# A two-layer decoder on one core: which VectorE instruction the sums of the experts are queued behind in linear attention

## The chip, the cores and the metric

The kernel runs on one core of one Trainium2 chip. The metric is the device time of one execution in microseconds; the time before is the median of three runs. Engines are named as the profile names them: PE is TensorE (PEld its weight loads), DVE is VectorE, ACT is ScalarE, POOL is GpSimd, SP is SyncE, which here only issues DMAs.

## The reference

A decoder of two layers works on x of 16 batch items, 256 positions and 256 features, in float32. Each of its six sublayers adds to x a function of the layer-normalised x:

```python
x = x + _L0_attn_ref(_layernorm(x, axis=-1), ...)    # causal softmax attention
x = x + _L0_xattn_ref(_layernorm(x, axis=-1), ctx_1024, ctx_1024, ...)
x = x + _L0_ffn_ref(_layernorm(x, axis=-1), ...)     # 8 experts, the best 2 of each token
x = x + _L1_attn_ref(_layernorm(x, axis=-1), ...)    # linear attention
x = x + _L1_xattn_ref(_layernorm(x, axis=-1), ctx_1024, ctx_1024, ...)
x = x + _L1_ffn_ref(_layernorm(x, axis=-1), ...)     # gated experts in the values and the output
```

The change lies where the third meets the fourth. The third ends with a sum: each token adds the outputs of its two experts, weighted. The fourth is linear attention with 16 heads of 16 features and the feature map phi(x) = elu(x) + 1:

```python
q, k, v = (_phi(qkv[0]), _phi(qkv[1]), qkv[2])
# for each position t:
S = S + k_t[..., :, None] * v_t[..., None, :]
z = z + k_t
out_t = einsum('bhde,bhd->bhe', S, q_t) / maximum(sum(z * q_t), 1e-6)
```

The kernel computes the same as a causal product: scores q k over all earlier positions, without a softmax, times v, divided by the row's sum.

## The kernel before

The program is one long unrolled sequence. x stays in SBUF as sixteen tiles `xs[b]` of 128 partitions by 2 by 256. Stages follow one another: attention and cross attention (layer 0), the experts (72 tiles of 128 gathered tokens, each result written to the DRAM tensor `yd`), then linear attention, cross attention and gated experts (layer 1). TensorE's instructions stand in the order in which the program writes them (`tc.manual_schedule`); those of the other engines are put in order by a scheduler when the program is built, by their dependences and its own estimate of when each is ready. Every engine's queue is then fixed, and each instruction waits there for its inputs. `tc.issue_after(i)` adds, to each instruction written in its block on the engine of `i`, the demand that it stands behind `i` in that queue. It adds no other dependence; instructions of the block on other engines are free.

Linear attention runs in steps s. A batch item b has four, one for each `(m, o)`: m is a half of the heads, o every second head of it, so step s works on item s // 4. `step3` writes, in this order: the scores of step s (`scores3`, L1014); the product with the values of step s - 2 (`weighted3`, L1030 and L1035); the transposition and division of step s - 3 (`finish3`, L1046 and L922 to L924); in even steps `project3` for step s + 2 (L197), which makes queries and keys for two steps; in steps 4b + 1 the transposition of the scaled rows of item b + 1 (`rows3`, L972) and the output projection of item b - 2 (`output3`); in steps 4b + 2 `combine(b + 2)`; in steps 4b + 3 the transposition of the result of item b - 1 (`out_T`) and the values of item b + 1 (`values3`). Into this the program fills the keys and values that cross attention needs later, made from the context (`context4`, the tile `c` loaded at L79 by SP, results stored by SP at L296 and L303): eight pieces ahead of the first step, three in each step before 0, and one in each later step.

Three pieces touch the change.

- `combine(b)` gathers, for each half t of item b and each of its two experts r, the rows of `yd` into a tile `y` (an indirect DMA issued by POOL, L949, four buffers), adds them weighted to `xs[b]` on DVE (L953, four sums), takes the statistics (L142, L143), the reciprocal standard deviation in twelve small instructions (L171 and L152 to L160), and scales the rows into `h` (L962, two instructions). `rows3(b)` reads `h`.
- `project3(b, m)` multiplies into PSUM, ACT takes exponential and relu of it (L998, L999), DVE forms `qk = min(ex, 1) + relu` (L1000), which is phi, and ACT makes the masked keys `ks` from it (L1003).
- `scores3` writes two PSUM tiles `sc`, of which there are two in all, so the next step's scores need both emptied: ACT copies one whole (L1023) and the middle of the other (L1022), DVE masks the rest of the other (L1021), and POOL later masks the first in SBUF (L1024).

A fourth piece is moved by it. `load_ffn` is written after step 10: two POOL copies (L895) that read a few elements of `xs[2]`, and behind them twelve SP loads of the last stage's weights (L899, L902).

Before, the block of `combine` is put behind the last instruction of the previous `combine`:

```python
with ExitStack() as order:
    if last:
        order.enter_context(tc.issue_after(last[-1]))
    ...
last.append(done.ins)
```

Of the kernel before, what the change touches and what calls it, by code (L numbers as in the profile page):

```python
# [13 lines left out]
ALU = mybir.AluOpType  # L14
# [11 lines left out]
def decoder(ctx: ExitStack, tc: tile.TileContext, a: dict, out: bass.AP):  # L26
# [3 lines left out]
    nc = tc.nc  # L30
# [108 lines left out]
    def stats(layer, b, pool):  # L139
        st = pool.tile([P, 2, 6], F32, tag="bnst", name="bnst", bufs=2)  # L140
        for t in range(2):
            nc.vector.bn_stats(st[:, t, :], xs[b][:, t, :])  # L142
            nc.vector.bn_aggr(mvs[layer][:, 2 * b + t, :], st[:, t, :])  # L143
# [22 lines left out]
    def rstd_one(layer, b, pool, eng=nc.vector):  # L166

        if layer not in rstds:
            rstds[layer] = const.tile([P, NT], F32, tag=f"rstd{layer % 2}", name=f"rstd{layer}")
        v = pool.tile([P, 2], F32, tag=f"rs_v{layer % 2}", name="rs_v", bufs=2)  # L170
        nc.vector.tensor_scalar(v, mvs[layer][:, 2 * b : 2 * b + 2, 1], 1e-5, None, ALU.add)  # L171
        rsqrt(rstds[layer][:, 2 * b : 2 * b + 2], v, pool, eng)
# [21 lines left out]
    def two_k(ps, lhsT, rhs):  # L194

        for c in range(2):
            nc.tensor.matmul(ps, lhsT=lhsT(c), rhs=rhs(c), start=(c == 0), stop=(c == 1))  # L197
# [731 lines left out]
    with ExitStack() as st:  # L929
# [2 lines left out]
        stats_tile(3)  # L932
        stats_tile(4)
        hs3, hTs, ons, qks, ats, oss = {}, {}, {}, {}, {}, {}
        last = []

        def mm3(shape, name):
            return psum.tile(shape, F32, tag="mm", name=name, bufs=4)

        def combine(b):  # L940

            with ExitStack() as order:
                if last:
                    order.enter_context(tc.issue_after(last[-1]))
                for t in range(2):
                    i = 2 * b + t
                    for r in range(2):
                        y = pool.tile([P, D], F32, tag="y", name="y", bufs=4)
                        nc.gpsimd.indirect_dma_start(  # L949
                            out=y, out_offset=None, in_=yd,  # L950
                            in_offset=bass.IndirectOffsetOnAxis(ap=rows[:, i, r : r + 1], axis=0),
                        )
                        nc.vector.scalar_tensor_tensor(  # L953
                            xs[b][:, t, :], y, gates[:, i, r : r + 1], xs[b][:, t, :],
                            ALU.mult, ALU.add,
                        )
                stats(3, b, pool)
                rstd_one(3, b, pool)
                h = hs3[b] = hp.tile([P, 2, D], F32, tag="h", name="h")
                for t in range(2):  # L960
                    i = 2 * b + t
                    done = nc.vector.tensor_scalar(  # L962
                        h[:, t, :], xs[b][:, t, :], mvs[3][:, i, 0:1], rstds[3][:, i : i + 1],
                        ALU.subtract, ALU.mult,
                    )
            last.append(done.ins)

        def rows3(b):
            ps = mm3([P, 2, S], "ps_hT")
# [20 lines left out]
        def project3(b, m):  # L990
            ps = mm3([P, 2, S], "ps_qk")
            for i in range(2):
                cols = slice(i * D + m * P, i * D + (m + 1) * P)
                two_k(ps[:, i, :], lambda c: wlqk[:, c, cols], lambda c: hTs[b][:, c, :])

            ex = pool.tile([P, 2, S], F32, tag="ex", name="ex", bufs=1)
            qk = pool.tile([P, 2, S], F32, tag="qk", name="qk", bufs=2)
            nc.scalar.activation(ex, ps, AF.Exp)  # L998
            nc.scalar.activation(qk, ps, AF.Relu)  # L999
            nc.vector.scalar_tensor_tensor(qk, ex, 1.0, qk, ALU.min, ALU.add)  # L1000
            ks = pool.tile([P, 2, S], F32, tag="ks", name="ks", bufs=2)
            for i in range(2):
                nc.scalar.mul(ks[:, i, :], qk[:, 1, :], halves[:, i : i + 1])  # L1003
            qks[b, m] = qk, ks

        def scores3(b, m, o):
            qk, ks = qks[b, m]
            at = ats[b, m, o] = pool.tile([P, 4, 3, P], F32, tag="at", name="at", bufs=3)
            scs = [psum.tile([P, 2, 512], F32, tag="sc", name="sc", bufs=2) for _ in range(2)]
            for cols, out_cols in ((slice(0, S), slice(0, S)), (slice(P, S), slice(S, S + P))):  # L1010
                k0 = cols.start
                for j in range(4):
                    part = slice(32 * j, 32 * j + 32)
                    nc.tensor.matmul(  # L1014
                        scs[j // 2][:, j % 2, out_cols], lhsT=ks[part, o, k0 : k0 + P],
                        rhs=qk[part, 0, cols], start=True, stop=True,
                    )
            sc3 = [x[:, :, 0:384].rearrange("p j (a q) -> p j a q", a=3) for x in scs]
            tri = tri3[:, 0::2, :].unsqueeze(1).to_broadcast([P, 2, 2, P])

            nc.vector.tensor_tensor(at[:, 0:2, 0::2, :], sc3[0][:, :, 0::2, :], tri, ALU.mult)  # L1021
            nc.scalar.copy(at[:, 0:2, 1, :], sc3[0][:, :, 1, :])  # L1022
            nc.scalar.copy(at[:, 2:4], sc3[1])  # L1023
            nc.gpsimd.tensor_tensor(at[:, 2:4, 0::2, :], at[:, 2:4, 0::2, :], tri, ALU.mult)  # L1024
# [55 lines left out]
        def step3(s):  # L1080
            def at_(k):
                return SETS[k] if 0 <= k < len(SETS) else None

            if at_(s):
                scores3(*SETS[s])
            if at_(s - 2):
                weighted3(*SETS[s - 2])
            if at_(s - 3):
                finish3(*SETS[s - 3])
            b = s // 4  # L1090
            if s % 2 == 0 and at_(s + 2):
                project3(*SETS[s + 2][:2])
            if s % 4 == 1:
                if b + 1 < NB:
                    rows3(b + 1)
                if b - 2 >= 0:
                    output3(b - 2)
            if s % 4 == 2 and 0 <= b + 2 < NB:
                combine(b + 2)
            if s % 4 == 3:  # L1100
                if 0 <= b - 1 < NB:
                    out_T(b - 1)
                if b + 1 < NB:
                    values3(b + 1)

        with tc.manual_schedule(engines={mybir.EngineType.PE}):
            next(late[0])
            next(late[1])
            combine(0)
            fill(late, 8)  # L1110
            for s in range(-3, len(SETS) + 6):
                step3(s)
                fill(late, 3 if s < 0 else 1)
                if s == 10:
                    load_ffn(xs[2][0:1, 0, 0:32])
# [391 lines left out]
```

## Time and profile before

| what | value |
|---|---|
| median of three runs | 3912.89 us (3911.7 to 3913.84) |
| profiled execution | 3917.66 us, span 3916.0 us |
| granted TensorE clock, mean | 0.983 |
| DVE busy in the span | 57% |
| last matmul of the experts to first scores of linear attention | 2016.7 to 2064.28 us |
| scores of step 0 to step 12 | 2064.28 to 2127.65 us |
| step 16 to step 56 | 2145.80 to 2341.50 us |
| ACT waiting for L1000, 2100 to 2350 us | 53.3 us in 25 waits |
| L1000 | 32 instructions, median 0.69 us |
| L953 | 64 instructions, median 0.48 us, longest 1.49 us |

Times within the kernel are microseconds from the start of the span. In a line of the timeline the first number is the start, the second the length, then engine, source line, operation, output and inputs; `x8` counts instructions that were merged, and what stands in square brackets is how long the engine had been idle and what ended that. In the chain of waits each piece is what the next one had to wait for. The clock is the share of full speed that TensorE was granted in a stretch.

### The profile page before, as it was taken

What the parts mean: (1) busy time and instruction counts of PE and PEld (TensorE: products, weight loads), DVE (VectorE), ACT (ScalarE), POOL (GpSimd) and SP (SyncE); (2) the same over time, 40 slices, a digit from 0 to 9 for tenths busy, and PEclk for the clock granted to TensorE, in tenths of its full rate; (3) what the DMA queues carried; (4) which work ended last, traced back from release to release, by engine and by line L of the source; (5) the groups of instructions that cost most, each with busy time, mean ns of one, the idle gap of its engine ahead of it and who ended that gap; (6) DMA issues with size and microseconds to landing.
All of it is one profiled execution on the core that took longest, in us unless ns stands there. A gap on an engine that the chain in (4) does not pass through costs nothing.

```text
span 3916.0 us, 63635 instructions
## 1 busy us (share of the span) xinstructions
PE 3759.0 (96%) x23088; PEld 2679.1 (68%) x23088; DVE 2248.7 (57%) x6215; ACT 1616.7 (41%) x4876; POOL 1039.2 (27%) x1472
## 2 busy tenths in 40 slices
PE   8999999999999999979989888998999999999999
PEld 6777776777777776756667665665666666666666
DVE  5666667645556555522234765776655555555554
ACT  4555554555555555423335555665212212212211
POOL 3332332333344334322224653221100000000000
PEclk9999999999999999979999999999999999999999
DMA  5000000010000000032234001001222222222222
GB/s 192 1 1 1 1 1 1 1 57 17 9 17 17 17 9 17 17 89 65 64 122 146 28 17 35 25 26 24 56 64 58 65 64 58 65 64 58 66 63 49
DMA packets 88456, 171.65 MB, mean 44 GB/s; under 512 B 12480, under 2 KB 60744, under 8 KB 79952
## 3 DMA queue, kind: packets, MB, share of 16 engines
q1 hardware_dynamic: 78992, 148.65, 13.9%
q0 software_dynamic: 8576, 17.87, 1.7%
q8 instruction: 186, 3.05, 0.3%
q10 hardware_dynamic: 576, 1.05, 0.1%
q14 instruction: 126, 1.03, 0.1%
HBM read 139.70 MB, written 27.82 MB: 43 GB/s over the span
## 4 chain that ended last, share of the span: by engine, by line
PE 86%; DVE 9%; issue 2%; ACT 1%; DMA 1%; POOL 1%; SPq 0%; another core or an unknown queue 0%; ACTq 0%; DVEq 0%; POOLq 0%
PE ps_qk L197 14%; PE po L1412 11%; PE ps_ve L197 11%; PE ps_v L197 6%; PE tr L266 6%; PE po L503 6%; PE sc L235 4%; PE ps_h L197 3%; PE po L877 3%; PE av L272 3%; PE sc L431 2%; PE av L488 2%; PE sc L1231 2%; PE sc L1205 2%; PE zt L1244 1%
## 5 line engine op out<-in xcount | busy, mean ns | idle before, releaser
L256 POOL TENSOR_TENSOR pr<-pr,sm 128x256 f32<-128x256 f32 (+1 forms) x384 | 309.7, 827 | 1444.2 <-DVE sm L254 1337.5
L250 ACT ACTIVATE pr<-sc,nmx 128x128 f32<-128x128 f32 (+1 forms) x768 | 314.7, 417 | 348.1 <-DVE nmx L248 311.9
L1412 PE MATMUL po<-w_oe,ut 128*128 128x256 f32 x2048 | 452.4, 379 | 0.0
L197 PE MATMUL ps_ve<-w_ve,hT 128*128 128x512 f32 x1024 | 450.8, 593 | 0.0
L1412 PEld LDWEIGHTS po<-w_oe,ut 128*128 128x128 f32 x2048 | 388.8, 190 | 52.8 <-issue 0.2
L267 ACT COPY pT<-tr 128x512 f32<-128x512 f32 (+1 forms) x256 | 135.9, 531 | 650.2 <-PE tr L266 650.2
L266 PEld LDWEIGHTS tr<-ident,pr 128*128 128x128 f32 x2176 | 270.8, 141 | 168.5 <-issue 117.5
L266 PE MATMUL tr<-ident,pr 128*128 128x128 f32 x2176 | 346.8, 275 | 14.1 <-ACT zT L497 11.2
L452 POOL TENSOR_TENSOR pr<-pr,sm 128x512 f32<-128x512 f32 x256 | 264.2, 1053 | 286.8 <-DVE sm L450 176.4
L446 ACT ACTIVATE pr<-sc,nmx 128x256 f32<-128x256 f32 x512 | 236.7, 470 | 250.8 <-DVE nmx L441 172.3
L197 PEld LDWEIGHTS ps_ve<-w_ve,hT 128*128 128x128 f32 x1024 | 191.1, 190 | 215.3 <-issue 207.1
L1384 DVE TENSOR_TENSOR tv<-ps_ve,gm 128x512 f32<-128x512 f32 x256 | 176.4, 689 | 204.7 <-PE ps_ve L197 198.2
L441 DVE CUSTOM_DVE_ANT_0 sc<-sc,mk 128x256 f32<-128x256 f32 x512 | 211.0, 443 | 112.6 <-PE sc L431 59.5
L248 DVE TENSOR_REDUCE nmx<-sc 128x2 f32<-128x256 f32 (+1 forms) x384 | 208.2, 556 | 111.0 <-ACT pr L250 106.2
L197 PE MATMUL ps_qk<-hT,w_a 128*128 128x256 f32 x1024 | 260.0, 387 | 0.0
L267 DVE COPY pT<-tr 128x384 f32<-128x384 f32 (+1 forms) x384 | 223.0, 594 | 19.2 <-PE tr L266 12.9
L197 PEld LDWEIGHTS ps_qk<-hT,w_a 128*128 128x128 f32 x1024 | 180.8, 191 | 29.7 <-issue 11.8
L197 PE MATMUL ps_qk<-hT,w 128*128 128x256 f32 x768 | 194.0, 398 | 0.0
L866 DVE COPY hs<-ps_h 128x512 f32<-128x512 f32 x72 | 49.8, 691 | 223.0 <-PE ps_h L197 223.0
L1211 DVE TENSOR_REDUCE nm<-sc 128x4 f32<-128x1024 f32 x128 | 150.9, 1221 | 43.2 <-PE sc L1205 43.2
L235 PE MATMUL sc<-qk 64*128 64x128 f32 (+1 forms) x1536 | 163.4, 346 | 8.6 <-ACT qk L417 6.2
L197 PEld LDWEIGHTS ps_qk<-hT,w 128*128 128x128 f32 x768 | 147.5, 203 | 19.4 <-issue 1.2
(279 smaller groups left out, 7010.4 us busy)
## 6 DMA issues: line engine op xcount, KB each, us to landing
gr<-gd SPq DMA_DIRECT2D x128, 512.0 KB
yd<-y SPq DMA_DIRECT2D x72, 128.0 KB
c<-in_ctxT SPq DMA_DIRECT2D x32, 256.0 KB
m_w<-in_m_w SPq DMA_DIRECT2D x16, 512.0 KB
x<-in_x SPq DMA_DIRECT2D x16, 256.0 KB
mk<-in_mask SPq DMA_DIRECT2D x16, 256.0 KB
hd<-h SPq DMA_DIRECT2D x16, 256.0 KB
w_ve<-in_f_ve SPq DMA_DIRECT2D x8, 512.0 KB
```

The lines of the kernel that those rows point to most:

```text
L197: nc.tensor.matmul(ps, lhsT=lhsT(c), rhs=rhs(c), start=(c == 0), stop=(c == 1))
L235: nc.tensor.matmul(sc[:, j, at : at + ks], lhsT=qk[rows, 0, qs], rhs=qk[rows, 1, 0:ks], start=True, stop=True,)
L248: nc.vector.tensor_reduce(nmx[:, qt, :], sc[:, :, sl], AX.X, ALU.max, negate=True)
L250: nc.scalar.activation(pr[:, j, sl], sc[:, j, sl], AF.Exp, bias=nmx[:, qt, j : j + 1], accum_out=sm[:, qt, j : j + 1],)
L256: nc.gpsimd.tensor_tensor(pr[:, :, sl], pr[:, :, sl], sm[:, qt, :].unsqueeze(2).to_broadcast([P, 2, n]), ALU.mult,)
L266: nc.tensor.transpose(tr[:, at : at + P], src, ident)
L267: copy(pT, tr[:, 0 : P * len(blocks)])
L441: nc.vector.tensor_tensor_reduce(out=sc[:, j, t, :], in0=sc[:, j, t, :], in1=mk[:, t, :], scale=-1.0, scalar=3.4e38, op0=ALU.add, op1=ALU. ...
L446: nc.scalar.activation(pr[:, j, t, :], sc[:, j, t, :], AF.Exp, bias=nmx[:, j, t : t + 1], scale=-1.0, accum_out=sm[:, j, t : t + 1],)
L452: nc.gpsimd.tensor_tensor(pr[:, j], pr[:, j], sm[:, j, :].unsqueeze(2).to_broadcast([P, 2, S]), ALU.mult)
L503: nc.tensor.matmul(po, lhsT=zTs[l, b, c][:, t * P : (t + 1) * P], rhs=wts[l][3][:, c, :], start=(c == 0), stop=(c == 7),)
L1412: nc.tensor.matmul(po[:, t, :], lhsT=ut[:, e, t * P : (t + 1) * P], rhs=woe[hp][:, e, :], start=(hp == 0 and e == 0), stop=(hp == 3 and e ...
```

## The change

`combine` is no longer put behind the previous `combine`. Each `project3` notes its DVE instruction L1000 in a list, `features`, and `combine` puts all its DVE instructions behind the newest one in that list at the time when it is written. In step 4b + 2 `project3(b + 1, 0)` is written just before `combine(b + 2)`, so the four sums, the statistics and the scalings of item b + 2 stand behind the queries and keys of item b + 1, half 0. `combine(0)` is written ahead of every `project3` and has nothing to stand behind; `combine(1)` follows `project3(0, 0)`. Nothing is computed otherwise, and no tile or buffer changes.

```diff
         hs3, hTs, ons, qks, ats, oss = {}, {}, {}, {}, {}, {}
-        last = []
+        features = []
...
         def combine(b):
             with ExitStack() as order:
-                if last:
-                    order.enter_context(tc.issue_after(last[-1]))
+                if features:
+                    order.enter_context(tc.issue_after(features[-1]))
...
-                    done = nc.vector.tensor_scalar(
+                    nc.vector.tensor_scalar(
                         h[:, t, :], xs[b][:, t, :], mvs[3][:, i, 0:1], rstds[3][:, i : i + 1],
                         ALU.subtract, ALU.mult,
                     )
-            last.append(done.ins)
...
-            nc.vector.scalar_tensor_tensor(qk, ex, 1.0, qk, ALU.min, ALU.add)
+            feature = nc.vector.scalar_tensor_tensor(qk, ex, 1.0, qk, ALU.min, ALU.add)
...
             qks[b, m] = qk, ks
+            features.append(feature.ins)
```

## The prediction

> **What bounds the kernel now.** I read the page first (busy times, clock by slice), then busy time by stretch for the linear-attention stage, then the chain of waits and the timeline inside it.
>
> ```profile
> PE 3759.0 (96%) x23088; PEld 2679.1 (68%) x23088; DVE 2248.7 (57%) x6215; ACT 1616.7 (41%) x4876; POOL 1039.2 (27%) x1472
> PE   8999999999999999979989888998999999999999
> PEclk9999999999999999979999999999999999999999
> ```
>
> TensorE is the bound: 96% busy. A change on VectorE can only pay where TensorE waits. Slice 20 and slices 22 to 24, counted from 0 (1958 to 2056 and 2154 to 2447 us, in and around linear attention), are among the few that show less than 9.
>
> ```profile
> 2017.20:2064.28 47.08, 37.12 (x156) 30.59 (x156) 21.65 (x87) 13.81 (x23) 19.80 (x22) 0.89 0.75 243
> 2064.28:2145.80 81.52, 77.43 (x736) 59.41 (x735) 41.50 (x126) 46.76 (x98) 34.33 (x49) 1.00 0.41 140
> 2145.80:2341.50 195.70, 174.19 (x1761) 128.91 (x1761) 137.78 (x482) 107.14 (x231) 116.58 (x195) 0.94 0.09 26
> ```
>
> Columns: stretch, length, busy PE, PEld, DVE, ACT, POOL, clock, DMA share, GB/s. The head of the stage has 10 us of idle PE, steps 0 to 15 have 4, and the ten blocks (of four steps, one per batch item) after them 21.5, with the clock at 0.94. So there are two losses. The head first (timeline of SP's queue, then of PE):
>
> ```profile
> 2036.63 0.32 SPq L296 DMA_DIRECT2D kd<-k  x1
> 2044.70 0.38 SPq L899 DMA_DIRECT2D w_ve<-in_f_ve  x1
> 2045.17 0.42 SPq L303 DMA_DIRECT2D vd<-v  x1
> 2045.68 0.38 SPq L79 DMA_DIRECT2D c<-in_ctxT  x1
> ...
> 2051.28 3.75 PE L197 MATMUL ps_k<-c,w 128*128 128x256 f32 x8 [8.44 <-DMA c<-in_ctxT]
> ```
>
> SP stands for 8 us at L899, the load of the last stage's weights. Its gate is two GpSimd copies (L895, 2044.44) that read batch item 2 after its sums, behind gathers on POOL. The context load queued behind it goes out at 2045.68, and PE waits 8.44 us for it; the clock then halves. The repeating loss (chain of waits; then DVE and PE timeline):
>
> ```profile
> 2180.66 0.17 DVE rstd L160
> 2180.90 0.29 issue
> 2181.19 0.41 DVE h L962
> 2181.60 0.39 DVE x L953
> 2181.99 0.61 DVE qk L1000
> 2182.65 0.39 issue
> 2183.05 0.49 ACT ks L1003
> 2183.54 0.69 ACT at L1023
> 2184.27 1.19 PE sc L1014 x12
> ...
> 2181.91 0.69 DVE L1000 SCALAR_TENSOR_TENSOR qk<-ex,qk 128x512 f32<-128x512 f32 x1
> 2183.30 0.69 DVE L1021 TENSOR_TENSOR at<-sc,tri 128x512 f32<-128x512 f32 x1
> 2184.27 0.97 PE L1014 MATMUL sc<-qk,ks 32*128 32x256 f32 x12 [2.19 <-ACT at L1023]
> ```
>
> ScalarE had ex and relu ready at 2179.05; L1000 ran at 2181.91, behind the chain rstd, h, x of a `combine`. ScalarE's `ks` waits for it, its two copies of `sc` stand behind `ks`, and the next scores need the PSUM these free. Restarts of L1014 with 2.0 to 2.4 us of idle come eleven times, steps 16, 20, ... 56.
>
> **What the Trainium skill says.** "TensorE: Matmul & The Clock Gate", Part 1, has the clock watched in a free-running window of 3413 ns and halved after an idle one. The trace agrees on the size (0.50 from 2186.1 to 2189.4; drops at 2223.55 and 2244.03 are six windows apart) but shows it after partly idle windows. Placing windows on that grid, those with 1.59 us idle or more dropped, those with 1.43 or less did not. A drop costs 1.7 us: steps of 5.64 against 3.75 and 4.01. The same part calls VectorE, ScalarE and GpSimd strict FIFO; every timeline above agrees. "SBUF — State Buffer", section on the two separate sides, says GpSimd and a VectorE instruction with two SBUF inputs exclude each other for a whole instruction. The trace agrees: at 2177.95 a 0.16 us L157 takes 1.19 while GpSimd's 1.27 us mask runs.
>
> **The change part by part.** No instruction is added or removed. `combine(b+2)` on VectorE (4 sums, statistics, 12 small ones, 2 scalings) now follows the L1000 last written, that of item b+1, m=0, instead of the previous `combine`. In the built order PE is the same. On DVE items 1 to 3 no longer stand ahead of the first L1000, and each later `combine` stands whole between one L1000 and the next. On SP no weight load comes before `vd` of item 11; all sixteen context loads but two precede them. POOL's gathers move the same way, still at least one block ahead of use.
>
> *Head.* The weights' gate needs item 2's sums, now after step 2's L1000, so SP no longer stops at 2036.63. The context load leaves when its buffer is free (2037.7); earlier ones took 4.3 to 5 us to use, PE needs it at 2042.84: no idle, or a few tenths. L1000 follows its ACT at 2042.94 instead of 2049.67. Gain 8.44, and the slow clock after it (3.75 + 2.62 against 2 x 1.89 us) 2.6: 11.0 us. Item 1's sums move behind L1000 and end near 2049.5; the step that needs them is near 2059. What is late next: the weights leave near 2075 (item 2's sums near 2070, then four gathers), 4 MB ahead of context item 14 and 7 MB ahead of 15. At the 328 GB/s that 2060 to 2080 shows now, these land near 2089 and 2098; PE asks near 2092 and 2103. I take zero cost; at 250 GB/s it would be about 2 us.
>
> *Step 12* (PE 6.01 us, 4.19 unstalled): the wait of 1.55 us is at L1003 behind the same DVE chain; gain 1.8.
>
> *Blocks.* Unstalled steps are 3.75, 4.19, 3.75, 4.19 (2351.32 on): 15.88 us; the measured mean is 19.57. Take t=0 at the scores of a step 4b+2 (2174.05). `x` plus output projection and its statistics fill DVE to 2.4, the mask of this step to 3.1. PE's ps_qk ends at 3.8, ACT's ex and relu at 5.0, L1000 5.0 to 5.7 (was 7.9). Now four sums (1.66), two statistics (0.75) and an aggregate (0.16) come before the next mask L1021: 8.2 to 8.8 (was 9.3 to 9.9). ACT's last copy ends near 9.25 (was 10.44). PE was free at 8.0, so it still idles 1.3 us: the wait moves from L1000 to the mask. GpSimd's twelve small operations (2.5 to 5.8) share the port with L1000 and the sums; I add 0.4 from the gaps between dependent sums, so 1.7. The rest of the combine (13 small at 0.16 to 0.20 with three of the normalisation between, 2.6; scalings 0.7) ends near 12.6, and that step's mask at 13.2 against PE ready at 13.5: 0.1 to 0.3 more. GpSimd's mask, behind three gathers of 1.25, ends near 14.4, about when PE wants it: 0 to 0.4. VectorE work per block is 14 us, so it is not the bound, but has little slack. I take 15.88 + 1.6 + 0.3 = 17.8 us. With 1.6 us at the clock's edge, I take a drop in four of ten blocks, 0.7: 18.5. Gain 1.1 a block, eleven blocks: 12 us. Bounds: no lock and no drop, 17.4, gain 24; a drop always, 19.5, gain 1; a GpSimd mask taking the port amid the sums (+1.3), loss 13.
>
> *Sum.* 11.0 + 1.8 + 12 = 25 us. The profiled execution took 3917.66 us, span 3916.0 (1.7 around it): span after, 3891. Its own time stands 4.8 above the median of the runs, 3912.89; taking the same difference off, 3888.
>
> **The rivals.**
> - *Only the head pays.* The clock drops in nearly every block and the stall stays at 1.8. For it: the tiny matmuls after a stall leave little reserve before 1.59 us. Against: 1.3 us without lock delays. 11 + 1.8 + 1 = 14: 3899.
> - *The clock never drops and no lock bites*: 37 us, 3876. For it: GpSimd's operations are mostly small at that point.
> - *Cancelled.* GpSimd's 1.27 us mask takes the port between two dependent sums each block, as at 2071.02, where four sums take 2.68 instead of 1.66 us: 13 lost, 13 won: 3913.
> - *Slower.* The port is lost twice a block, once in the sums, once in the small chain (as at 2177.95), so both masks are late. The block is 15.88 + 3.0 + 1.4 + 1.7 = 22.0, 2.4 more than now, 26 over eleven blocks, less 13: 3926. It decides once a block loses 4.9 us or more (3.7 now, 1.2 from the head's share).
> - *The order doesn't act*: excluded, the built queue shows it.
>
> **How the numbers follow.** Forecast 0.50; only the head 0.25; clock never drops 0.12; cancelled 0.07; slower 0.06. Predicted 3888 us. The range from the clean case to "only the head" with 4 us for contended loads is 3873 to 3903; the last two cases and tails lie outside. A change of 0.2%, 7.8 us, is what can be told from none. Faster: all of the first three, 0.87; same 0.07; slower 0.06.
>
> **What would show it.** Right: no idle of PE over 1 us near 2043 and SP not stopped at L899; L1000 within 0.1 us of relu; `ACT ks <- DVE qk` (53.3 us in 2100 to 2350) down to under 25; PE restarts at steps 16, 20, ... led by the mask L1022 instead, 1.3 to 1.8 us each; clock above 0.94. Wrong: restarts of 2.5 us or more, sums over 2.2 us for four, PE waiting for `c` near 2090 to 2105, or a block over 19.6 us.

## The result, and the profile after

The changed kernel takes 3943.08 us (median of four runs, 3942.5 to 3945.61) against 3913.15 us for the kernel before on the same chip (four runs, 3911.7 to 3913.84): a ratio of 1.0078, 95% interval 1.0062 to 1.0094. It is 30 us slower, where the forecast was 25 us faster.

The page of the kernel after, busy times and granted clock by slice:

```profile
PE 3778.1 (96%) x23088; PEld 2693.5 (68%) x23088; DVE 2292.3 (58%) x6215; ACT 1617.8 (41%) x4876; POOL 1035.5 (26%) x1472
...
PEclk9999999999999999989999899999999999999999
```

DVE is busy for 43.6 us more than before with the same 6215 instructions. No instruction was added, so some of them take longer. Busy time by stretch, the same three as before:

```profile
2017.20:2064.28 47.08, 44.27 (x263) 36.40 (x261) 15.86 (x52) 21.81 (x41) 13.78 (x14) 1.00 0.57 187
2064.28:2145.80 81.52, 74.80 (x694) 55.89 (x688) 57.48 (x167) 42.71 (x91) 38.89 (x56) 0.93 0.49 169
2145.80:2341.50 195.70, 162.10 (x1511) 117.24 (x1504) 144.55 (x402) 91.57 (x196) 99.82 (x174) 0.91 0.08 23
```

The head is repaired: PE is busy for 44 of 47 us (37 before) at full clock. (The stage starts 4.1 us earlier in this execution, so the same times hold somewhat later work; the head's own length follows below.) The third stretch, blocks only, is worse: 34 us of idle PE instead of 21.5, clock 0.91 instead of 0.94, and 1511 matmul records instead of 1761 in the same time. Where PE stands still (timeline of PE, the head and one block):

```profile
2025.48 1.97 PE L197 MATMUL ps_k<-c,w 128*128 128x256 f32 x8 [1.23 <-DMA c<-in_ctxT]
2048.68 1.97 PE L197 MATMUL ps_k<-c,w 128*128 128x256 f32 x8 [1.23 <-DMA c<-in_ctxT]
...
2183.34 0.92 PE L1015 MATMUL sc<-qk,ks 32*128 32x256 f32 x12 [1.46 <-ACT at L1023]
2190.73 1.65 PE L1015 MATMUL sc<-qk,ks 32*128 32x256 f32 x12 [2.95 <-ACT at L1023]
```

(From the diff on, lines stand one lower than before: the sums are L954, scores L1015, DVE's mask L1022, GpSimd's mask L1025; L1000 stays.) The stop of 8.44 us is gone. Each block now stands still twice, at the scores of steps 4b+4 and 4b+5, where before it stood once for 2.0 to 2.4 us; and 1.65 us for twelve small matmuls is the half clock. What stands behind the two stalls is told by the chain of waits through this block; each piece is what the next one waited for:

```profile
2178.27 0.04 DVE qk L1000
...
2178.88 0.55 DVE x L954 x2
2179.43 0.24 issue
2179.67 1.89 DVE x L954 x2
...
2182.31 0.57 DVE at L1022
...
2184.02 1.87 DVE rsq_t L159
...
2186.49 1.83 DVE rsq_k L160
...
2189.67 0.61 DVE at L1022
2190.28 0.02 issue
2190.30 0.38 ACT at L1023
2190.68 0.04 issue
2190.73 1.43 PE sc L1015 x7
```

The wait moved as forecast, from L1000 to DVE's masks. But three pieces are far too long: the sums, and two operations on 128 x 2 elements that take 0.16 us elsewhere. Now the same stretch on POOL and DVE (timeline):

```profile
2179.37 1.51 POOL L1025 TENSOR_TENSOR at<-at,tri 128x512 f32<-128x512 f32 x1
...
2183.59 0.95 POOL L950 DMA_INDIRECT y<-yd,rows  x1 [0.30 <-DVE rsq_k L152]
2184.55 1.29 POOL L1025 TENSOR_TENSOR at<-at,tri 128x512 f32<-128x512 f32 x1
2186.01 0.98 POOL L950 DMA_INDIRECT y<-yd,rows  x1 [0.16 <-DVE rsq_t L159]
2187.01 1.27 POOL L1025 TENSOR_TENSOR at<-at,tri 128x512 f32<-128x512 f32 x1
...
2178.88 2.68 DVE L954 SCALAR_TENSOR_TENSOR x<-y,gates,x 128x256 f32<-128x256 f32 x4
...
2184.02 1.86 DVE L159 SCALAR_TENSOR_TENSOR rsq_t<-rsq_t,rs_v 128x2 f32<-128x2 f32 x1
...
2186.49 1.82 DVE L160 SCALAR_TENSOR_TENSOR rsq_k<-rsq_t,rsq_k 128x2 f32<-128x2 f32 x1
```

Each long one ends within 0.04 us of the end of a GpSimd mask, or has one in its middle. The mask of step 4b+2 stands behind the twelve small operations of the previous output projection in GpSimd's queue and so falls on the sums (2.68 us against 1.66 in the head, at 2039.07). Those of steps 4b+3 and 4b+4 stand behind three and four gathers and fall on the chain of small operations. That is 1.0 + 1.7 + 1.7 = 4.4 us of DVE in each block.

Where the 30 us lie, with a block measured as the distance between two output transposes (L1058 before, L1059 after) on PE: eleven blocks have a mean of 19.61 us before and 23.08 after, which makes 38.2 us of loss. From the first expert gather (2019.62 before, 2015.53 after) to the first of these blocks it is 121.65 us before and 115.71 after: the head gains 9.6 up to the first scores, and 3.7 of that are lost again ahead of the first block; the new stalls begin there, in step 13. 38.2 - 5.9 = 32.3 us; the profiled execution before started the stage 4.1 us later, as it was itself 4.5 above its median, and the two spans differ by 27.8. Part of the 38 us is the clock: its mean over the eleven blocks is 0.94 before and 0.91 after, from which I estimate that half clock cost 13 and 23 us.

### The profile page after: what moved, and what is told of

The parts are those of the page before. It is cut to its first block, busy times and chain, and to the rows that moved or that the text cites. A ratio compares the mean times of both kernels' runs of the same rounds, so it can differ in the third digit from the quotient of the medians.

```text
span 3943.8 us, 63611 instructions
## 1 busy us (share of the span) xinstructions
PE 3778.1 (96%) x23088; PEld 2693.5 (68%) x23088; DVE 2292.3 (58%) x6215; ACT 1617.8 (41%) x4876; POOL 1035.5 (26%) x1472
## 4 chain that ended last, share of the span: by engine, by line
PE 85%; DVE 10%; issue 1%; ACT 1%; DMA 1%; POOL 1%; SPq 0%; ACTq 0%; DVEq 0%; POOLq 0%
PE ps_qk L197 14%; PE po L1413 11%; PE ps_ve L197 11%; PE ps_v L197 6%; PE tr L266 6%; PE po L503 6%; PE sc L235 4%; PE ps_h L197 3%; PE po L877 3%; PE av L272 2%; PE sc L431 2%; PE av L488 2%; PE sc L1206 2%; PE sc L1232 2%; PE zt L1245 1%
## 5 line engine op out<-in xcount | busy, mean ns | idle before, releaser
L1404 DVE TENSOR_TENSOR ut<-gr,av 128x1024 f32<-128x1024 f32 x128 | 155.3, 1214 | 5.1 <-PE av L277 5.1
```

## The experiments

Two theories were open at first. *Port*: DVE loses the shared SBUF port to GpSimd's masks, because the new order brings sums and chain under them. *Length*: a whole combine is too long to stand between two masks of DVE, whatever GpSimd does. And the head's gain was to be checked by itself. The kernel before was timed with every set of kernels (medians 3913.2 to 3914.3 us). All times:

| kernel | us | ratio to before, 95% | mean block, us |
|---|---|---|---|
| before | 3913.15 | | 19.61 |
| after | 3943.08 | 1.0062 to 1.0094 | 23.08 |
| new order for items 1 to 3 alone | 3906.13 | 0.9974 to 0.9988 | 19.73 |
| new order from item 4 on alone | 3955.76 | 1.0094 to 1.0128 | 22.97 |
| before, weights gated later | 3908.90 | 0.9979 to 0.9993 | 19.73 |
| after without GpSimd's masks | 3872.65 | 0.9881 to 0.9914 | 17.33 |
| before without GpSimd's masks | 3887.69 | 0.9915 to 0.9948 | 17.43 |
| after, gathers a block late | 4002.33 | 1.0211 to 1.0245 | 27.2 |
| after, masks earlier | 3893.88 | 0.9932 to 0.9965 | 18.76 |
| after, gathers alone behind the mask | 3916.75 | 0.9997 to 1.0014 | 20.70 |
| after, small operations alone behind | 3944.08 | 1.0063 to 1.0096 | 22.95 |
| before, masks earlier | 3910.72 | 0.9983 to 1.0000 | 18.46 |
| masks earlier, combine cut in two | 3888.66 | 0.9917 to 0.9950 | 18.25 |
| the same, gathers two and two | 3882.00 | 0.9903 to 0.9936 | 17.71 |

### Which half loses

```diff
+                behind = features if b < 4 else last
-                if features:
-                    order.enter_context(tc.issue_after(features[-1]))
+                if behind:
+                    order.enter_context(tc.issue_after(behind[-1]))
```

and the other half with `last if b < 4 else features`.

> Only the combines of items 1 to 3 stand behind the newest queries and keys; from item 4 on each stands behind the combine before it, as in the kernel before. Theory A (the head's gain is real, the blocks are what loses): 3900 to 3904 us, about 11 below the kernel before; the step to the first scores without an idle of PE over 1.3 us, blocks of about 19.6 us with one restart of 2.0 to 2.4 us each. Rival H (the head's gain in the changed kernel was only its earlier start in that one execution, about 4 us, or is given back to the weights' later load): 3909 to 3914.

> The other half: items 1 to 3 as in the kernel before, from item 4 on behind the newest queries and keys. Theory A: all of the loss and none of the gain, 3950 to 3956 us, blocks of 22 to 24 us with two stalls of the scores each (about 1.5 and 2.9 us). Rival H (the weights' load, which the changed kernel moved into the first blocks, has a share in the loss): 3925 or less.

Measured: 3906.13 and 3955.76 us. Theory A holds in sign for both, and in size for the second: the head alone wins 7.1 us, the blocks alone lose 42.5. The head's stop is gone here too (from the first gather to the first scores 33.4 us, 44.7 before), which is 11.3 us; but farther on, at 2097.08, one L1000 (L1003 in this kernel) takes 2.50 us instead of 0.69: a GpSimd mask runs from 2097.74 to 2099.01, right behind a gather. The `ks` that needs it waits 2.56 us, a copy of `v` stands behind that on ScalarE, and PE idles 2.69 us near 2101. The forecast for this kernel, 3900 to 3904, missed by 2; this one idle is enough for it.

### What makes the head's stop

```diff
-                    load_ffn(xs[2][0:1, 0, 0:32])
+                    load_ffn(xs[4][0:1, 0, 0:32])
```

> The kernel before, its order on VectorE kept; only the two copies that gate the last stage's weights read batch item 4 instead of item 2, so that SP comes to these loads later. Theory S (the head's loss is SP's stop at the weights, which holds back a context load): PE's idle of 8.4 us near 2043 is gone, 3902 to 3907 us, as with the head alone. Rival D (it is VectorE, where three combines stand ahead of the first newest queries and keys): an idle of 5 us or more stays in the head, 3910 to 3914.

3908.90 us, between the two ranges. SP no longer stops at the weights, and the 8.44 us become, in the timeline of PE:

```profile
2049.95 3.78 PE L197 MATMUL ps_v<-w,c 128*128 128x256 f32 x8 [4.12 <-ACT k L295]
```

ScalarE's copy of `k` stands there behind `ks` (L1003), which waited 8.37 us for L1000, behind two combines on DVE. So two things held PE up in the head, one hidden behind the other: SP's queue, and beneath it 4.1 us of DVE's order. The new order takes away both and reaches further than the gate alone: 35.0 us from first gather to first scores, 40.6 with the late gate.

### GpSimd's masks left out

```diff
-            nc.gpsimd.tensor_tensor(at[:, 2:4, 0::2, :], at[:, 2:4, 0::2, :], tri, ALU.mult)
```

in the kernel after and, as a control, in the kernel before. Half of the heads are left without the causal mask.

> The changed kernel without GpSimd's multiplication by the causal mask, so that half of the heads are left unmasked. Theory P (VectorE loses the shared port to GpSimd's masks): four sums 1.7 us instead of 2.7, none of the twelve small operations of the chain over 0.3 us instead of two of 1.8, second stall of a block under 0.5 us, block 16.5 to 18 us: 3875 to 3890 us. Rival G (the gathers hold the port as well): small operations of 0.8 to 1.2 us remain beside the gathers, second stall about 1.5 us: 3905 to 3920. Rival L (it is the length of the combine between two masks, not the port): both stalls stay within 0.5 us of 1.5 and 2.9: 3930 or more.

> The kernel before without GpSimd's multiplication by the causal mask (half of the heads unmasked): the control to the same omission in the changed kernel, 3872.65 us. Theory P (the new order would have paid as forecast if GpSimd's masks took nothing from VectorE): the kernel before gains only the 1.0 us that its first small operation loses in each block and some clock, 3895 to 3903 us, so that the change is worth about 25 us here, as in the sum of the prediction. Rival N (without the masks the order brings nothing): within 5 us of 3873.

3872.65 and 3887.69 us. The omission is worth 70 us in the kernel after and 27 in the kernel before. The kernel after comes out 2 us below the range of theory P. The length theory falls: with the whole combine still between the same two instructions of DVE the stalls are 0.45 and nothing. The kernel after without masks, groups by shape over the blocks:

```profile
L954 DVE SCALAR_TENSOR_TENSOR x<-y,gates,x 128x256 f32<-128x256 f32 x36 | 15.0, 479 | 0.0
...
L159 DVE SCALAR_TENSOR_TENSOR rsq_t<-rsq_t,rs_v 128x2 f32<-128x2 f32 x29 | 4.7, 161 | 1.0
...
L160 DVE SCALAR_TENSOR_TENSOR rsq_k<-rsq_t,rsq_k 128x2 f32<-128x2 f32 x19 | 3.1, 162 | 0.7
```

The last two columns are the mean of one in ns and the idle before. The mean of a sum is 479 ns (731 in the kernel after), that of L159 161 (725) and of L160 162 (987). The four gathers still run beside the chain here, and no operation is long: rival G falls too, a gather by itself does not hold VectorE up.

The control meets neither of its expectations: it is 7 us faster than the first one's range (3895 to 3903), and not within 5 us of 3873. Without masks the blocks are 17.33 us in the new order and 17.43 in the old: the order on VectorE, to which the prediction gave 12 us, is worth 0.1 us a block. What the old order lost in its blocks, 19.61 against 17.43, came with a mask as well. In the kernel before, on POOL and DVE:

```profile
2177.70 0.20 POOL L162 TENSOR_TENSOR rsq_t<-rsq_t,rs_v 128x2 f32<-128x2 f32 x1
2177.85 1.27 POOL L1024 TENSOR_TENSOR at<-at,tri 128x512 f32<-128x512 f32 x1
2179.09 0.19 POOL L163 TENSOR_SCALAR rsq_t<-rsq_t 128x2 f32<-128x2 f32 x1
...
2177.95 1.19 DVE L157 TENSOR_TENSOR rsq_t<-rsq_k 128x2 f32<-128x2 f32 x1
```

It stands between GpSimd's small operations and falls on one L157 per block (1.19 us for 0.16), just ahead of h, x and L1000. That is 1.0 of the 2.2 us; the rest fits the clock, whose mean over the blocks is 0.94 with the masks and 1.00 without (an estimate: 6% of 19.6 us is 1.2). Nearly all of the 15 us between these two kernels lies ahead of the blocks.

### The masks put earlier, first wrongly

```diff
+                if masks:
+                    order.enter_context(tc.issue_after(masks[-1]))
                 for t in range(2):
...
-            nc.gpsimd.tensor_tensor(at[:, 2:4, 0::2, :], at[:, 2:4, 0::2, :], tri, ALU.mult)
+            mask = nc.gpsimd.tensor_tensor(at[:, 2:4, 0::2, :], at[:, 2:4, 0::2, :], tri, ALU.mult)
+            masks.append(mask.ins)
```

and `rstd_one(4, b, pool, nc.gpsimd)` inside `issue_after(masks[-1])`.

> The changed kernel with another order on GpSimd alone: the twelve small operations after the output projection stand behind the mask of that step, the four gathers of a combine behind the mask of their step. VectorE's and TensorE's orders stay. Theory P (only the masks' coincidence with the sums and the small chain costs): sums 1.7 us, no small operation over 0.3, second stall under 0.5, block 16.5 to 18 us: 3875 to 3895 us. Rival G (gathers hold the port too): the chain still runs beside the four gathers and keeps one or two operations of about 1 us: second stall 1 to 2 us, 3905 to 3925. Rival L (length): within 10 us of the changed kernel, 3933 or more.

4002.33 us, which no theory expected (3933 or more, of rival L, meant a kernel within 10 us of the changed one). The fault is the edit's own. The gathers of a combine run one block ahead of it; put behind the mask of the combine's own step they come too late, and the sums (L957 in this kernel and the next) wait for them. The waits of the whole stage say so:

```profile
DVE x L957 <- DMA y<-yd,rows: 88.9, 31, 4.6
```

(us in total, times, longest.) The run tells nothing of the theories, except that a chain with no mask near it again has only operations of 0.16 us.

### The masks earlier, with the gathers left a block ahead

```diff
+                if len(masks) > 3:
+                    order.enter_context(tc.issue_after(masks[-4]))
                 for t in range(2):
...
             stats(4, b, pool)
-            rstd_one(4, b, pool, nc.gpsimd)
...
+            if s % 4 == 2 and b - 2 >= 0 or s == len(SETS) + 5:
+                with tc.issue_after(masks[-1]):
+                    rstd_one(4, b - 2, pool, nc.gpsimd)
```

> The changed kernel with GpSimd's order alone changed, this time with each gather left a block ahead of its sums: the gathers behind the mask of the step before them (4b+3), the twelve small operations behind the mask of step 4b+2. VectorE's and TensorE's orders stay. Theory P: four sums 1.7 to 2.0 us, no small operation of the chain over 0.4 us, the stall of step 4b+5 under 0.5 us, that of 4b+4 about 0.5: 3873 to 3888 us. Rival L (length of the combine): stalls stay at 1.5 and 2.9, 3935 or more. Rival M (the masks take the port from something else instead, the next queries and keys or the scalings): one stall of 1.5 us or more is left in each block, 3900 to 3920.

3893.88 us: 49 us less than the changed kernel with the same combine at the same place on VectorE, and 20 less than before. The groups by shape over the blocks:

```profile
L957 DVE SCALAR_TENSOR_TENSOR x<-y,gates,x 128x256 f32<-128x256 f32 x40 | 16.7, 478 | 0.0
...
L159 DVE SCALAR_TENSOR_TENSOR rsq_t<-rsq_t,rs_v 128x2 f32<-128x2 f32 x30 | 4.8, 161 | 1.0
...
L160 DVE SCALAR_TENSOR_TENSOR rsq_k<-rsq_t,rsq_k 128x2 f32<-128x2 f32 x20 | 3.2, 162 | 0.7
```

Sums and chain are free, with all masks computed. The theory of the port stands, and in the blocks it is the order on GpSimd that decides. The time is 6 us above the upper end of what was expected: blocks are 18.5 us (the last is 21.3) instead of 17.3, with stalls of 0.46 and 0.35, and ScalarE waits 0.3 us in most blocks for a GpSimd mask, which was not priced.

### One half of that order each

The gathers alone:

```diff
+                if len(masks) > 3:
+                    order.enter_context(tc.issue_after(masks[-4]))
```

and the small operations alone:

```diff
-            rstd_one(4, b, pool, nc.gpsimd)
...
+            if s % 4 == 2 and b - 2 >= 0 or s == len(SETS) + 5:
+                with tc.issue_after(masks[-1]):
+                    rstd_one(4, b - 2, pool, nc.gpsimd)
```

> The changed kernel with only the gathers behind the mask of step 4b+3; GpSimd's twelve small operations stay ahead of the mask of step 4b+2, which so still falls on the sums. Theory P, priced from the trace of the changed kernel: sums 2.7 us (1.0 lost), chain free, the stall of step 4b+5 gone or under 0.5, that of 4b+4 about 1.5: 3900 to 3915 us. If the gathers alone carry the whole loss: within 5 us of 3894. If the small operations do: 3930 or more.

> The other half: only the twelve small operations behind the mask of step 4b+2, the gathers as in the changed kernel, ahead of the masks of steps 4b+3 and 4b+4. Theory P: sums 1.7 us, the chain still has two operations of about 1.8 us, stalls about 0.5 and 2.9: 3922 to 3938 us. If the small operations carry the loss: 3900 or less. The two halves' losses against the kernel with both should add up to about 49 us, if they don't hide one another.

3916.75 and 3944.08 us, each above its range, by 2 and by 6 us. Against the changed kernel that is -26 and +1, and -49 with both. The halves don't add up. With the gathers alone moved (sums L957, scalings L966, GpSimd's masks L1028), from the timeline:

```profile
2167.45 2.92 POOL L1028 TENSOR_TENSOR at<-at,tri 128x512 f32<-128x512 f32 x2
...
2174.36 0.96 POOL L953 DMA_INDIRECT y<-yd,rows  x1 [0.30 <-DVE rsq_t L157]
2175.32 1.29 POOL L1028 TENSOR_TENSOR at<-at,tri 128x512 f32<-128x512 f32 x1
...
2166.96 3.69 DVE L957 SCALAR_TENSOR_TENSOR x<-y,gates,x 128x256 f32<-128x256 f32 x4
...
2174.59 2.19 DVE L966 TENSOR_SCALAR h<-x,mv,rstd 128x256 f32<-128x256 f32 x2
```

Two masks instead of one now fall on the sums (3.69 us), and the third on the scalings (2.19 instead of 0.74): my pricing had left 1.0 us there, and it is 2.0 + 1.5. With the small operations alone moved the sums take 1.66 us, the stall of step 4b+4 falls from 1.46 to 0.45, but the chain keeps its two long operations (1.97 and 1.81) and the stall of 2.94, and the blocks shorten by 0.1 us only. The clock did not take the difference; it is 0.91 in both. The trace shows where the mask of step 4b+2 went instead (POOL, DVE, PE):

```profile
2173.03 1.26 POOL L1026 TENSOR_TENSOR at<-at,tri 128x512 f32<-128x512 f32 x1 [3.96 <-ACT at L1025]
...
2173.09 1.23 DVE L152 TENSOR_SCALAR rsq_k<-rs_v 128x2 int32<-128x2 int32 x1
...
2174.80 1.71 PE L1016 MATMUL sc<-qk,ks 32*128 32x256 f32 x16
```

It falls on L152 (0.17 elsewhere), which stands ahead of DVE's own mask, and the scores of step 4b+3 stretch from 0.94 to 1.71 us. So about 0.8 of the 1.0 us that the sums won is lost a step earlier. A mask that is pushed off one operation is caught by the next unless there is room for it.

### The old order on VectorE with the masks earlier

The same move of `rstd_one(4, ...)` in the kernel before, and its gathers, which run two blocks ahead:

```diff
                 if last:
                     order.enter_context(tc.issue_after(last[-1]))
+                if len(masks) >= 8:
+                    order.enter_context(tc.issue_after(masks[-8]))
```

> The kernel before with the same hand on GpSimd's order as in the kernel with the masks earlier: the twelve small operations behind the mask of step 4b+2, the gathers (which here lie two blocks ahead of their combine) behind that of step 4b+3. VectorE's order in the blocks stays that of before. It asks how much of the 20 us that the masks-earlier kernel won belongs to VectorE's new order. If the masks are all that either order loses: the small operation of 1.19 us goes to 0.16, block about 18.3 us, 3897 to 3903 us, and the new order on VectorE is worth about 5 us. If VectorE's new order carries the gain, as the prediction had it: 3907 us or more. If the old order is the better one once the masks are out of the way: 3893 or less.

3910.72 us, which falls under the sentence "VectorE's new order carries the gain", but not for its reason. The blocks are 18.46 us, as the first branch had them, and even 0.3 shorter than with the new order and masks earlier, although a mask now falls on another operation of the chain in each block (L171, 0.95 us instead of 0.17, at 2177.09). Of the 12.7 us won there (11 x 1.15), 8.3 are lost ahead of them: the head's stop is still there (8.46 us), and there are new stalls of 2.90 near 2088 and of 1.70 near 2127 with half clock. So it agrees with the two kernels without masks that VectorE's order hardly matters in the blocks by itself; for the total it doesn't separate the two, since the edit changed the first steps as well (one combine's four sums and one's four gathers stand later there).

### A better order

Sums and statistics behind DVE's mask of step 4b+2, small chain and scalings behind that of step 4b+3; then also two gathers behind the mask of step 4b+3 and two behind that of 4b+4. The moves on GpSimd are those of the masks-earlier kernel.

```diff
-                    order.enter_context(tc.issue_after(features[-1]))
+                    order.enter_context(tc.issue_after((firsts or features)[-1]))
...
                 stats(3, b, pool)
+
+        def scale(b):
+            with ExitStack() as order:
+                if firsts:
+                    order.enter_context(tc.issue_after(firsts[-1]))
                 rstd_one(3, b, pool)
...
-            nc.vector.tensor_tensor(at[:, 0:2, 0::2, :], sc3[0][:, :, 0::2, :], tri, ALU.mult)
+            first = nc.vector.tensor_tensor(at[:, 0:2, 0::2, :], sc3[0][:, :, 0::2, :], tri, ALU.mult)
+            firsts.append(first.ins)
```

and for the gathers two and two:

```diff
-                if len(masks) > 3:
-                    order.enter_context(tc.issue_after(masks[-4]))
                 for t in range(2):
                     i = 2 * b + t
+                    if len(masks) > 3:
+                        order.enter_context(tc.issue_after(masks[t - 4]))
```

> As the kernel with the masks earlier on GpSimd, and VectorE's combine cut in two: sums and statistics behind the first mask of step 4b+2, the chain of small operations and the scalings behind that of step 4b+3. If the stall left over comes from the sums standing ahead of the mask, it goes: 3865 to 3880 us. If the sums then hold up the newest queries and keys, and with them ScalarE's copies, by about 1.3 us: no better than with the masks earlier alone, 3875 to 3895 us.

> The kernel with the combine cut in two (3888.7 us), and of its four gathers two behind the mask of step 4b+3 and two behind that of 4b+4, so that the mask of 4b+4 no longer stands behind all four and no longer runs into the newest queries and keys (1.85 us there instead of 0.69). If that wait is what is left in the block: 0.6 to 0.8 us a block less, 3878 to 3884 us. If the mask then falls on something else: 3887 or more.

3888.66 us for the cut, in the range of its second branch; the intervals of this and of the uncut version overlap, though each of its four runs is below each of the uncut version's (5 us in the medians). The mask of step 4b+4, behind four gathers, falls on an L1000 in every block (1.85 us at 2172.90): mean 1124 ns. L1009 is L1000 in these two kernels. With the gathers two and two, 3882.00 us, in the expected range; L1000 in the groups of that kernel:

```profile
L1009 DVE SCALAR_TENSOR_TENSOR qk<-ex,qk 128x512 f32<-128x512 f32 x21 | 14.2, 679 | 14.0 <-ACT ex L1007 9.7 <-ACT qk L1008 4.3
```

Blocks of 17.58 us with one stall of 0.36, close to the 17.33 without masks. Masks still fall on DVE in each block, on an L157 of the chain (1.27 us at 2162.46) and on an L152 (1.22 us at 2172.87), but now no stall of PE over 0.36 us follows, outside the last block. This version is 31 us faster than the kernel before and 61 faster than the change as it stands.

## Why the prediction was wrong

- *Head, 11.0 us: right in mechanism and nearly in size.* Only half of the 8.44 us was SP's alone; the late gate left 4.1 us, which were DVE's order, and the change takes away both. SP does not stop, L1000 starts at 2038.46 right behind the relu (2037.84 + 0.59), and the head is 9.6 us shorter in the kernel after, 11.3 with the head alone. The largest idle is 1.23 us where "a few tenths" stood. The zero for the later weight loads held: no wait for `c` over 1.23 us.
- *Step 12, 1.8 us*: its wait is gone, but step 13 brings the first of the new stalls (1.84 us, half clock), so it did not stay.
- *Blocks, a gain of 12 us: the step that failed.* It came out as a loss of 38. The failed terms are two. First, "GpSimd's twelve small operations (2.5 to 5.8) share the port with L1000 and the sums; I add 0.4": this term was to price the port, and what DVE lost measures 4.4 us a block. It counted only the small operations; of the masks it asked when they end, at a cost of 0 to 0.4, and not what they hold up meanwhile, except as one of the bounds ("amid the sums (+1.3)"). The mask of step 4b+2 moved in GpSimd's queue from between the small operations (2177.85 before) to behind all twelve (2179.37 after), onto the sums, and the masks of steps 4b+3 and 4b+4 fall on the chain. Second, the clock: 0.7 a block was added; with stalls of 1.46 and 2.95 us it is 0.91 over the blocks, about 2 us a block (an estimate, 9% of 23.08). With and without the masks the block is 23.08 and 17.33 us; of these 5.75 the clock's 2 leave 3.6 to the port, so not all of DVE's 4.4 reach TensorE. The clock's edge that the prediction read from the kernel before, 1.43 to 1.59 us of idle PE in a window, does not carry over: counted on the same grid of 3.413 us, the clock dropped in the kernel after behind windows with 1.47 us idle (from 2275.1 and 2343.4) and even 1.32 (from 2281.9 and 2350.2, each just behind half clock), and did not behind one with 1.59 (from 2326.3).
- *What the old blocks lost*: "3.7 now" was put down to L1000 standing behind the chain. The two kernels without masks show that 2.2 of the 3.7 came with the masks (their hold on L157 and the clock). The 1.19 us at L157 were shown in the prediction, as a proof of the lock, and not counted as the cause.
- *The unstalled model itself was good*: without masks the new order has 15.88 + 1.45 = 17.33 us a block, where 15.88 + 1.6 + 0.3 - 0.4 (the port) makes 17.4. (The prediction's 1.3 + 0.4 is 1.7, and its sum took 1.6.)
- *The signs*: `ACT ks <- DVE qk` went from 53.3 to 16.0 us in the same stretch, as said. The clock, 0.91, is under the 0.94 that was named, and restarts of 2.95 us, sums of 2.68 us and blocks over 19.6 are three of the four signs of a wrong forecast.
- *The rival that came true is "Slower"*, in its mechanism (the port lost in the sums and in the small chain, both masks late), with 3926 us and a chance of 0.06. It is short by 17: the port is lost three times a block, not twice, and each loss in the chain is 1.7 us and not 1.0.

"SBUF — State Buffer" in the Trainium skill, section on the two separate sides, has the lock held for the whole instruction, and for VectorE's two-port modes as well as for two SBUF inputs. In the traces one input was enough: with the small operations alone moved, a shift with a single input (L152, at 2173.09) took 1.23 us instead of 0.17 and ended 0.03 after the mask. Which mode it runs in, no trace shows.

## What to carry to other kernels

When a change reorders one engine, read the queue of the engine that shares a port with it as closely: here VectorE's new order by itself was worth 0.1 us a block (without the masks), and with that order where GpSimd's 1.27 us masks stand makes blocks of 18.8 or of 23.1 us. Price a port by the longest instruction that can meet a chain of dependent ones, at every place where the two may meet, and not by the average overlap. And when a trace shows an operation at seven times its length, count that first among the causes of the stall behind it.

## What was not expected of the hardware

- A mask right behind a gather holds VectorE from before its own recorded start. In all blocks of the kernel after (2131 to 2385 us), small operations that start 0.70 us or more ahead of such a mask run in 0.16 us, beside the gather; those that start 0.50 to 0.55 ahead end 0.02 to 0.04 us after the mask's end, 1.8 to 1.9 us in all (in the kernel with the small operations alone moved, also at 0.66). Where no gather stands ahead, an operation that started 0.15 us before the mask was not held. Why it is so was not tried, and the profile's times on POOL are rough, so the recorded starts may have a share in it.
- Not every VectorE instruction is held. Statistics took their usual 0.75 us for two beside a mask (2177.67, masks earlier, mask from 2177.29 to 2178.56), and instructions of 128x512 that read PSUM kept 0.69 (L1071 in eleven blocks of the kernel before, each started under a mask).
- Idle time alone does not tell when the clock halves. In the kernel after a stall of 2.93 us near 2331, which the grid of windows cuts in two, was followed by full clock, and one of 1.32 us near 2284 by half.
